# Opening each PSUM bank once, and adding the norm's transposes onto a shift that ACT writes

## The chip, the cores and the metric

The kernel runs on one core of a Trainium2 chip. The time is the device time of that core in microseconds (us); the median of several runs is given. The core's engines are PE (TensorE, matrix products and transposes), DVE (VectorE), ACT (ScalarE), POOL (GpSimd) and SP (SyncE, which issues the DMAs here). Each runs its own queue in order and waits for the others through semaphores. PE writes its results to PSUM, which has eight banks; POOL does not touch PSUM.

## The reference

The input `x` is 128 x 32 x 256 (batch, time, features), the condition 128 x 256. Two layers follow each other. All that the change touches is in the first, and in the norm at the head of the second:

```
# layer 0: a recurrence over the 32 time steps (RK4, state q and p of 128 x 256, q0 = p0 = cond)
dq = q - q**3/3 - p + x[:, t] + tanh(q) @ coupling.T + bias      # four times a step
dp = 0.08 * (q + 0.7 - 0.8 * p)
q, p = clip(q + DT/6*(dq1 + 2*dq2 + 2*dq3 + dq4)), clip(...)
# its FFN on every step's q: block-quantized, 256 -> 1024 -> 256
x1 = x + mx_linear(silu(mx_linear(q, w_gate)) * mx_linear(q, w_up), w_down)

# layer 1: norm with scale and shift from the condition, then attention and a ternary FFN
scale, shift = split(cond @ W_emb + b_emb, 2)                    # 128 x 256 each: per batch row
xn = x1 * rsqrt(mean(x1*x1) + 1e-6) * g_norm * (1 + scale) + shift
out = x1 + ffn1(attention(xn @ W_qkv))
```

The batch has 128 rows, so a time step's state fills the 128 partitions once.

## The kernel before, in words

**Phases.** Phase one goes over the 32 time steps: `step(t)` (line 604) is the recurrence, `ffn0(t)` (line 915) the first FFN and the norm of that step. Phase two goes over 32 groups of 128 tokens (`tokens(g)`, line 1134) and starts with products of `xnT`, the transposed norm that phase one leaves behind.

**Order of the work.** Nothing is issued where it is written. Each function calls `work.add(engine, cost, fn, reads, writes, ...)`; the class `Work` (lines 100 to 341) then plans all queues with these costs (list scheduling, run to and fro for up to 40 rounds, phase one first and then phase two from the engine times that phase one ends with), and `emit` (line 1366) issues the items in that order. Buffers (`Buf`) are given slots of a pool by the planner as they come free. `keep_warm` (line 321) looks for planned gaps of PE over 0.45 us and puts products of zeros (line 1375) into them, into a buffer whose first writer is a later item of PE.

**The recurrence in a step.** Four stages, each with an accumulator `ps[i]` in PSUM: `ps[0]` and `ps[2]` are the same slot, `ps[1]` and `ps[3]` the other; each slot has a bank of its own (line 413). A stage's accumulator is first opened by `opened` (line 519), a PE product of zeros with the start flag and no stop flag, 128 x 256 in bf16. Then DVE (`nest`, line 577) or, for the fourth, ACT (line 661) writes start values over it, and PE adds onto them: `plus` (line 612) adds a scaled buffer through a scaled identity, and `slope` has ACT compute tanh and square (lines 619, 620), PE the product with the coupling (line 626) and POOL the cube (line 633). DVE then reads the sum (`nest`, `add_sat`, line 672).

**The FFN and the norm of a step.** The state is transposed into `ps_turn` (line 551), quantized (lines 708, 929, 909 on DVE, 935 on POOL), turned by DMA (line 457), multiplied with gate and up (line 950), combined (958, 962), quantized again (708, 977, 909, 985), and turned by DMA. The down product goes into `po`, in a bank of its own: `opened(po)`, ACT writes the residual `x` (line 993), and eight products add onto it (line 997). ACT copies it out as `x1` (line 1003) and sums its squares (line 1009), POOL takes the power (line 1015). For the first 27 steps ACT then scales (line 1020), POOL multiplies with the gain (line 1024) and adds the shift (line 1028); for the last five (`LATE`) DVE does both (lines 1033, 1035). PE transposes the result into `px`, one of two slots in the bank `ps_turn` (line 1036), and ACT copies it into `xnT` (line 1038). The other users of `ps_turn` in each step are the state's transpose `pt` (line 920) and the transpose `pd` of the next `x` (line 591), which ACT reads (line 597).

**Gain and shift** are made once in `modulation` (line 823): PE multiplies the transposed condition with both halves of `W_emb` (line 831), and DVE adds the bias to each half (lines 837, 839).

Of the kernel before, what the change touches and what calls it, by code (L numbers as in the profile page):

```python
# [14 lines left out]
AF = mybir.ActivationFunctionType  # L15
# [5 lines left out]
P = 128  # L21
# [18 lines left out]
PE, DVE, ACT, POOL, SP = "PE", "DVE", "ACT", "POOL", "SP"  # L40
# [305 lines left out]
def kernel(  # L346
# [22 lines left out]
    nc = tc.nc  # L369
    B, T, N = x.shape  # L370
    FF = w0_gate.shape[0]
    NC = N // P
    FC = FF // P
# [22 lines left out]
    mid = slots("mid", HALF, 10)  # L396
    slim = slots("slim", N, 18)
# [8 lines left out]
    def banks(name, n, count):  # L406

        tiles = [ps_1.tile([P, HALF], F32, name=f"{name}{i}") for i in range(-(-count * n // HALF))]
        return [
            Slot(t[:, k : k + n], f"{name}{i}") for i, t in enumerate(tiles) for k in range(0, HALF, n)  # L410
        ][:count]

    ps_stage = [banks(f"ps_stage{i}", N, 1) for i in range(2)] * 2
    ps_po = banks("ps_po", N, 1)
    ps_sum = banks("ps_sum", N, 4)
    shared = ps_sum.pop()
    n_tiny = FF // BLOCK
# [7 lines left out]
    def fixed(name, shape, dtype=F32):  # L425

        b = Buf(())
        t = tile_of(name, shape, dtype)
        b.slots, b.slot = [Slot(t)], 0
        return b, t  # L430
# [30 lines left out]
    def two(ap):  # L461
        return ap.rearrange("p (c k) -> p c k", c=NC)

    def load(slots_, src, rank, as_=None, after=()):
        b = Buf(slots_)
        add(
            SP, 0.45, lambda: nc.sync.dma_start(as_(b.ap) if as_ else b.ap, src),
            fills=[b], rank=rank, tail=4.0 if slots_ is raws else 1.8, after=after,
        )
        return b  # L470
# [17 lines left out]
    b_oh, w_oh = fixed("w_oh", [P, NC, N])  # L488
    b_gp, g_prod = fixed("g_prod", [P, D_HEAD])
    b_gain, gain = fixed("gain", [P, N])  # L490
    b_shift, shift = fixed("shift", [P, N])
    b_xnT, xnT = fixed("xnT", [P, NC, B, T])
    xnT_flat = xnT.rearrange("p c b t -> p c (b t)")
    x1_dram = dram.tile([B, T, N], F32, name="x1_dram")
# [21 lines left out]
    zeros = tile_of("zeros", [P, N], BF16)  # L516
    nc.gpsimd.memset(zeros, 0.0)

    def opened(dst, rank, after=()):
        add(  # L520
            PE, 0.11,
            lambda: nc.tensor.matmul(dst.ap, lhsT=zeros[:, :P], rhs=zeros, start=True, stop=False),
            [], [dst], rank=rank, after=after,
        )


# [21 lines left out]
    def turn(dst, src, n=NC):  # L548
        for c in range(n):
            sl = slice(c * P, (c + 1) * P)  # L550
            nc.tensor.transpose(dst[:, sl], src[:, sl], ident)  # L551
# [52 lines left out]
    def step(t, q, p, d):  # L604
        rank = t - 500.0
        ps = [Buf(slots_) for slots_ in ps_stage]
        x, w, z = Buf(ps_sum), Buf(ps_sum), p
        q2, q3, m4, w2, qn = Buf(slim), Buf(slim), Buf(slim), Buf(slim), Buf(states)

        def plus(i, eye, src, cost=0.43):  # L610
            return add(
                PE, cost, lambda: nc.tensor.matmul(ps[i].ap, lhsT=eyes[eye], rhs=src.ap, start=False, stop=False),  # L612
                [src], [ps[i]], rank=rank,
            )

        def slope(i, qi):

            th, sq = Buf(slim), Buf(slim)
            add(ACT, 0.32, lambda: nc.scalar.activation(th.ap, qi.ap, AF.Tanh, scale=1.0 / S3 if i == 2 else 1.0), [qi], [th], rank=rank, table="silu")  # L619
            add(ACT, 0.31, lambda: nc.scalar.activation(sq.ap, qi.ap, AF.Square, scale=CUBES[i]), [qi], [sq], rank=rank)  # L620

            def mm():
                for c in range(NC):
                    for m in range(NC):
                        sl = slice(m * P, (m + 1) * P)
                        nc.tensor.matmul(  # L626
                            ps[i].ap[:, sl], lhsT=coup[i][:, c, sl], rhs=two(th.ap)[:, c, :],
                            start=False, stop=(c == NC - 1 and m == NC - 1),
                        )

            add(PE, 0.9, mm, [th, b_coup[i]], [ps[i]], rank=rank)
            add(
                POOL, 0.685, lambda: nc.gpsimd.tensor_tensor(sq.ap, sq.ap, qi.ap, MULT),  # L633
                [qi], [sq], rank=rank, port=True,
            )
            return sq

        for i in range(2):
            opened(ps[i], rank)
            nest(ps[i], p, -h / 2 * (1.0, P2[0])[i] * S / K[i], q, rank)  # L640
            if not i:
                started.append(work.items[-1])
            plus(i, i, d)
        nest(x, p, -h * P3[0] * S / K[2], q, rank)
        cube = slope(0, q)
        nest(w, p, LAST[0] * S / LAST[1], q, rank)
        nest(z, p, END[0] * S / END[1], q, rank)
        nest(q2, ps[0], K[0], cube, rank, SUB)
        plus(1, 1, q2)
        cube = slope(1, q2)  # L650
        opened(ps[2], rank)
        nest(ps[2], q2, -h * P3[2] / K[2], x, rank)
        plus(2, 2, d)
        nest(w, d, h / 6 / LAST[1], w, rank)
        nest(w2, w, LAST[1] / LAST[2], q2, rank)
        nest(z, z, END[1] / END[2], q2, rank)
        nest(q3, ps[1], K[1] * S3, cube, rank)
        plus(2, 6, q3)
        cube = slope(2, q3)
        opened(ps[3], rank)  # L660
        add(ACT, 0.27, lambda: nc.scalar.mul(ps[3].ap, w2.ap, LAST[2]), [w2], [ps[3]], rank=rank)
        plus(3, 4, q3)
        nest(z, z, END[2] / S, q3, rank)
        nest(m4, ps[2], -K[2], cube, rank, SUB)
        plus(3, 5, m4)
        cube = slope(3, m4)
        edge = ALPHA / BETA

        def add_sat(dst, in0, in1, low, high):
            add(  # L670
                DVE, 0.335,
                lambda: nc.vector._custom_dve(TENSOR_ADD_SAT, out=dst.ap, in0=in0.ap, in1=in1.ap, s0=high, s1=low),
                [b for b in (in0, in1) if b is not dst], [dst], rank=rank,
            )

        add_sat(z, z, m4, (CLAMP - edge) / S, (-CLAMP - edge) / S)
        add_sat(qn, ps[3], cube, -CLAMP, CLAMP)
        return qn, z
# [143 lines left out]

    def modulation(rank):
        emb = [load(mid, w_emb[c * P : (c + 1) * P, :], rank) for c in range(NC)]
        b_e = load(mid, b_emb.partition_broadcast(P), rank)
        g_n = load(slim, g_norm.partition_broadcast(P), rank)
        pe = Buf(ps_gu)

        def mm():
            for c in range(NC):  # L830
                nc.tensor.matmul(
                    pe.ap, lhsT=two(condT)[:, c, :], rhs=emb[c].ap, start=(c == 0), stop=(c == NC - 1)
                )

        add(PE, 1.72, mm, [b_condT, *emb], [pe], rank=rank)
        tt = nc.vector.tensor_tensor
        add(DVE, 0.335, lambda: tt(gain, pe.ap[:, :N], b_e.ap[:, :N], ADD), [pe, b_e], [b_gain], rank=rank)
        add(DVE, 0.335, lambda: stt(gain, gain, 1.0, g_n.ap, ADD, MULT), [g_n], [b_gain], rank=rank, port=True)
        add(DVE, 0.335, lambda: tt(shift, pe.ap[:, N:], b_e.ap[:, N:], ADD), [pe, b_e], [b_shift], rank=rank)

    def constants_of_phase_two(rank):

# [72 lines left out]
    def ffn0(t, q):  # L915
# [72 lines left out]
                [b8, bscl], fills=[bq], rank=rank, port=True,  # L988
            )
        turned(bT, bq, FF, rank)  # L990
        po, x1, ms, xn, px = Buf(ps_po), Buf(slim), Buf(tiny), Buf(slim), Buf(ps_turn)
        opened(po, rank)
        add(ACT, 0.31, lambda: nc.scalar.copy(po.ap, xt.ap), [xt], [po], rank=rank)

        def down():
            for c in range(FC):
                nc.tensor.matmul(
                    po.ap, lhsT=bT.ap[:, c * P : (c + 1) * P], rhs=w0dT[:, c, :],
                    start=False, stop=(c == FC - 1),
                )  # L1000

        add(PE, 0.88, down, [bT, b_w0d], [po], rank=rank)
# [15 lines left out]
        if t < T - LATE:  # L1018
            add(
                ACT, 0.42, lambda: nc.scalar.activation(xn.ap, po.ap, AF.Copy, scale=m1()),  # L1020
                [po, ms], [xn], rank=rank,
            )
            add(
                POOL, 0.685, lambda: nc.gpsimd.tensor_tensor(xn.ap, xn.ap, gain, MULT),
                [b_gain], [xn], rank=rank, port=True,
            )
            add(
                POOL, 0.685, lambda: nc.gpsimd.tensor_tensor(xn.ap, xn.ap, shift, ADD),
                [b_shift], [xn], rank=rank, port=True,
            )  # L1030
        else:
            add(
                DVE, 0.335, lambda: stt(xn.ap, po.ap, m1(), gain, MULT, MULT), [po, ms, b_gain], [xn], rank=rank
            )
            add(DVE, 0.335, lambda: tt(xn.ap, xn.ap, shift, ADD), [b_shift], [xn], rank=rank, port=True)
        add(PE, 0.22, lambda: turn(px.ap, xn.ap), [xn], [px], rank=rank)
        xnT_done.append(
            add(ACT, 0.4, lambda: nc.scalar.copy(xnT[:, :, :, t], two(px.ap)), [px], fills=[b_xnT], rank=rank)
        )
# [398 lines left out]
```

## Time and profile before

| | |
|---|---|
| Three runs | 836.7, 838.51, 838.08 us; median 838.08 |
| The profiled execution | span 839.5 us from the first to the last instruction; its time outside the span is not given |
| Phase one, to the last copy into `xnT` | 418.5 us |
| Phase two | 421.0 us |
| Busy over the span | PE 93%, DVE 86%, POOL 73%, ACT 60% |
| Products of zeros by `opened` | 160 (128 into the stages, 32 into `po`) |
| Products of zeros by `keep_warm` | 219 |

How to read it: a line such as `L1028 POOL TENSOR_TENSOR slim<-slim,shift` names the line of the kernel, the engine, the operation, and out<-in by buffer names without their numbers. `L577` is the helper `nest`, `L551` the helper `turn` and `L522` the products of `opened`. A matmul of fp32 operands is two records; a transpose is one. Matmuls overlap in time, so that a busy PE is not a PE at its limit. A wait line says which engine and line stood for which other.

### The profile page before, as it was taken

The numbers are of one execution on the slowest core, as the hardware profiler recorded it, in microseconds if no ns is written. First come the engines' busy times: TensorE is split into PE (matmuls) and PEld (weight loads), VectorE is DVE, ScalarE is ACT, GpSimd is POOL, SyncE is SP. The second block draws the span as 40 slices with busy tenths as digits, with TensorE's granted clock in tenths as the row PEclk, the third lists the DMA queues.
The fourth block names the chain that finished last, engine by engine and source line by source line (L and its number), as shares of the span: only waits on it lengthen the run. The fifth ranks groups of instructions, "written<-read, shape, count | busy, mean of one in ns | idle before, by whom it ended". The sixth has DMA issues, their size and how long they took to land.

```text
span 839.5 us, 26212 instructions
## 1 busy us (share of the span) xinstructions
PE 783.7 (93%) x10455; PEld 583.7 (70%) x10455; DVE 721.1 (86%) x1848; ACT 507.3 (60%) x1021; POOL 610.0 (73%) x956
## 2 busy tenths in 40 slices
PE   7889999999999999998688999999999999999996
PEld 4666677777777877775455576777767676778675
DVE  4998999999999999999368698979898889888794
ACT  3225456655656665696533676767668576765864
POOL 5787998988798988889555677785773877867320
PEclk9999999999999999999799999999999999999999
DMA  7312232323132343255300021133223122231333
GB/s 229 107 39 48 59 77 61 83 60 70 51 71 70 70 139 65 57 130 127 78 2 7 16 44 50 40 71 65 57 37 57 40 49 53 37 62 34 75 83 76
DMA packets 128891, 55.53 MB, mean 66 GB/s; under 512 B 102144, under 2 KB 127616, under 8 KB 128768
## 3 DMA queue, kind: packets, MB, share of 16 engines
q1 hardware_dynamic: 128768, 53.85, 28.0%
q8 instruction: 82, 1.34, 0.7%
q14 instruction: 41, 0.34, 0.1%
HBM read 21.32 MB, written 8.39 MB: 35 GB/s over the span
## 4 chain that ended last, share of the span: by engine, by line
PE 29%; DVE 17%; POOL 6%; ACT 5%; DMA 4%; issue 4%; ACTq 0%; SPq 0%; DVEq 0%; POOLq 0%
PE ps_two L1284 4%; PE ps_one L1146 4%; PE ps_two L1326 3%; DVE wide L1315 3%; DVE tiny L1092 2%; DMA wide_bf<-wide_bf 2%; PE ps_one L1228 2%; POOL wide L1315 2%; PE ps_one L1198 2%; PE ps_stage L626 2%; PE ps_one L1349 2%; PE ps_stage L612 2%; PE ps_two L551 2%; PE ps_one L1153 2%; DVE wide L1299 1%
## 5 line engine op out<-in xcount | busy, mean ns | idle before, releaser
L1315 POOL TENSOR_TENSOR wide<-wide 128x512 f32<-128x512 f32 x116 | 148.2, 1298 | 62.9 <-DVE wide L1315 24.8
L626 PEld LDWEIGHTS ps_stage<-slim,coup 128*128 128x128 f32 x1024 | 128.7, 192 | 19.0 <-ACT slim L619 11.2
L626 PE MATMUL ps_stage<-slim,coup 128*128 128x128 f32 x1024 | 139.2, 279 | 0.3
L633 POOL TENSOR_TENSOR slim<-slim,slim 128x256 f32<-128x256 f32 x96 | 72.6, 756 | 23.0 <-ACT slim L620 16.5
L612 PE MATMUL ps_stage<-slim,eye 128*128 128x256 f32 x256 | 80.0, 396 | 4.8 <-DVE slim L577 3.7
L619 ACT ACTIVATE slim<-slim 128x256 f32<-128x256 f32 x96 | 39.4, 410 | 51.7 <-DVE slim L577 51.7
L977 POOL TENSOR_TENSOR mid<-mid,tiny 128x512 f32<-128x512 f32 x64 | 66.6, 1050 | 4.8 <-DVE tiny L698 4.7
L985 POOL TENSOR_TENSOR wide_bf<-mid,tiny 128x512 bf16<-128x512 fp8e4 x64 | 66.9, 1051 | 4.1 <-DVE mid L909 3.9
L1326 PE MATMUL ps_two<-had_ffn,wide 128*128 128x128 f32 x512 | 63.7, 278 | 2.0 <-ACT wide L1321 1.1
L620 ACT ACTIVATE slim<-slim 128x256 f32<-128x256 f32 x96 | 39.1, 407 | 42.9 <-DVE slim L577 40.8
L1326 PEld LDWEIGHTS ps_two<-had_ffn,wide 128*128 128x128 f32 x512 | 60.3, 192 | 6.0 <-ACT wide L1321 2.6
L612 PE MATMUL ps_stage<-drives,eye 128*128 128x256 f32 x192 | 60.5, 398 | 2.8 <-DVE ps_stage L577 2.1
L1146 PE MATMUL ps_one<-w_qkv_sb,xnT 128*128 128x512 f32 x128 | 61.4, 603 | 0.4 <-ACT v_pad L1162 0.2
L1315 DVE TENSOR_TENSOR wide<-wide 128x512 f32<-128x512 f32 x76 | 57.4, 778 | 1.3 <-POOL wide L1315 1.3
L1292 ACT ACTIVATE mid<-ps_two,tiny 128x512 f32<-128x512 f32 x64 | 43.4, 687 | 23.7 <-PE ps_two L1284 23.3
L612 PEld LDWEIGHTS ps_stage<-slim,eye 128*128 128x128 f32 x256 | 39.5, 189 | 25.5 <-DVE slim L577 19.5
L1228 PEld LDWEIGHTS ps_one<-v_pad,mid 32*32 32x32 f32 x4096 | 40.8, 105 | 22.3 <-issue 17.4
L1299 DVE SCALAR_TENSOR_TENSOR wide<-ps_two,tiny,mid 128x512 f32<-128x512 f32 x64 | 46.9, 741 | 9.2 <-ACT mid L1292 8.5
L1334 ACT ACTIVATE wide<-ps_two,magic,tiny 128x1024 f32<-128x1024 f32 x32 | 38.6, 1205 | 26.0 <-DVE tiny L1100 21.8
L1228 PE MATMUL ps_one<-v_pad,mid 32*32 32x17 f32 x4096 | 46.7, 181 | 3.2 <-DVE mid L1221 1.8
L1092 DVE TENSOR_REDUCE tiny<-ps_two 128x1 f32<-128x1024 f32 x32 | 38.6, 1206 | 8.9 <-PE ps_two L1326 8.8
L962 DVE TENSOR_TENSOR mid<-ps_gu,mid 128x512 f32<-128x512 f32 x64 | 43.6, 682 | 2.3 <-PE ps_gu L950 1.7
(169 smaller groups left out, 2151.1 us busy)
## 6 DMA issues: line engine op xcount, KB each, us to landing
x_step<-in_x_dram SPq DMA_DIRECT2D x32, 128.0 KB, 2.1
x_add<-in_x_dram SPq DMA_DIRECT2D x32, 128.0 KB, 2.1
x_dram<-slim SPq DMA_DIRECT2D x32, 128.0 KB, 1.7
slim<-x_dram SPq DMA_DIRECT2D x32, 128.0 KB, 2.4
out_dram<-slim SPq DMA_DIRECT2D x32, 128.0 KB, 1.9
raws<-in_L_ffn_w_gate_dram SPq DMA_DIRECT2D x4, 512.0 KB, 4.8
raws<-in_L_ffn_w_up_dram SPq DMA_DIRECT2D x4, 512.0 KB, 6.1
raws<-in_L_ffn_w_down_dram SPq DMA_DIRECT2D x4, 512.0 KB, 5.0
```

The source lines that it names most:

```text
L612: PE, cost, lambda: nc.tensor.matmul(ps[i].ap, lhsT=eyes[eye], rhs=src.ap, start=False, stop=False),
L626: nc.tensor.matmul(ps[i].ap[:, sl], lhsT=coup[i][:, c, sl], rhs=two(th.ap)[:, c, :], start=False, stop=(c == NC - 1 and m == NC - 1),)
L633: POOL, 0.685, lambda: nc.gpsimd.tensor_tensor(sq.ap, sq.ap, qi.ap, MULT),
L962: DVE, 0.6, lambda act=act, it=it, pu=pgu[1]: tt(it.ap, pu.ap, act.ap, MULT),
L977: lambda it=it, ks=ks: nc.gpsimd.tensor_tensor(blocks(it.ap), blocks(it.ap), spread(binv.ap[:, ks], BLOCK), MULT),
L985: lambda b8=b8, ks=ks, sl=sl: nc.gpsimd.tensor_tensor(blocks(bq.ap[:, sl]), blocks(b8.ap), spread(bscl.ap[:, ks], BLOCK), MULT),
L1092: lambda: nc.vector.tensor_reduce(am.ap[:, 0:1], src.ap[:, :n], AX.X, ALU.max, apply_absolute_value=True),
L1146: nc.tensor.matmul(pqk.ap, lhsT=xnT_flat[:, c, tok], rhs=w_qkv_sb[:, c, : 2 * N], start=(c == 0), stop=(c == NC - 1),)
L1228: nc.tensor.matmul(by_v(po.ap)[row, hd, :], lhsT=by_head(exT.ap)[row, hd, :], rhs=v_pad.ap[row, hd, :], start=True, stop=True,)
L1299: lambda pgu=pgu, act=act, sl=sl: stt(it.ap[:, sl], pgu.ap[:, HALF:], sgu.ap[:, 1:2], act.ap, MULT, MULT),
L1315: eng.tensor_tensor(dv[:, :, e, :], sv[:, :, 0, :], sv[:, :, 1, :], op)
L1326: nc.tensor.matmul(pfh.ap[:, sl], lhsT=iT.ap[:, sl], rhs=had_ffn, start=True, stop=True)
```

## The change

1. `opened` goes, with its 160 planned products. Four products of zeros are issued ahead of all planned work instead: one for each of the two stage banks and one for each half of the `po` bank. The first three have the start flag; the fourth, in the same bank as the third, has not. The products that add onto these banks keep `start=False` and now have the stop flag.
2. `px` moves from a slot of `ps_turn` to the second half of the bank of `po`, where it has one slot of its own.
3. The shift is kept transposed (`[P, NC, B]`). In `modulation` PE makes it transposed with four products, ACT adds the bias (loaded one value to a partition by a small DMA), and the DVE addition goes; the bias that is broadcast to all partitions is only the gain's half.
4. In `ffn0` the addition of the shift on POOL or DVE goes. ACT copies the transposed shift into `px`, and the two transposes of the norm, with `start=False`, add onto it. The copy into `xnT` is as before.

```diff
-    ps_po = banks("ps_po", N, 1)
+    ps_po, ps_px = ([slot] for slot in banks("ps_po", N, 2))
...
-    b_shift, shift = fixed("shift", [P, N])
+    b_shift, shift = fixed("shift", [P, NC, B])
+    b_be, shift_bias = fixed("shift_bias", [P, NC])
...
-    def opened(dst, rank, after=()):
-        add(
-            PE, 0.11,
-            lambda: nc.tensor.matmul(dst.ap, lhsT=zeros[:, :P], rhs=zeros, start=True, stop=False),
-            [], [dst], rank=rank, after=after,
+    for slot in (ps_stage[0][0], ps_stage[1][0], ps_po[0], ps_px[0]):
+        nc.tensor.matmul(
+            slot.ap, lhsT=zeros[:, :P], rhs=zeros, start=slot is not ps_px[0], stop=True, skip_group_check=True
         )
...
-                PE, cost, lambda: nc.tensor.matmul(ps[i].ap, lhsT=eyes[eye], rhs=src.ap, start=False, stop=False),
+                PE, cost, lambda: nc.tensor.matmul(ps[i].ap, lhsT=eyes[eye], rhs=src.ap, start=False, stop=True, skip_group_check=True),
...
-                            start=False, stop=(c == NC - 1 and m == NC - 1),
+                            start=False, stop=True, skip_group_check=True,
...
         for i in range(2):
-            opened(ps[i], rank)
             nest(ps[i], p, -h / 2 * (1.0, P2[0])[i] * S / K[i], q, rank)
...
-        opened(ps[2], rank)
         nest(ps[2], q2, -h * P3[2] / K[2], x, rank)
...
-        opened(ps[3], rank)
         add(ACT, 0.27, lambda: nc.scalar.mul(ps[3].ap, w2.ap, LAST[2]), [w2], [ps[3]], rank=rank)
...
     def modulation(rank):
         emb = [load(mid, w_emb[c * P : (c + 1) * P, :], rank) for c in range(NC)]
-        b_e = load(mid, b_emb.partition_broadcast(P), rank)
+        b_e = load(slim, b_emb[:N].partition_broadcast(P), rank)
+
+        def load_shift_bias():
+            with nc.allow_non_contiguous_dma(reason="256 elements, one per partition and chunk"):
+                nc.sync.dma_start(shift_bias, b_emb[N:].rearrange("(c p) -> p c", p=P))
+
+        add(SP, 0.45, load_shift_bias, fills=[b_be], rank=rank, tail=1.8)
...
-                    pe.ap, lhsT=two(condT)[:, c, :], rhs=emb[c].ap, start=(c == 0), stop=(c == NC - 1)
+                    pe.ap[:, :N], lhsT=two(condT)[:, c, :], rhs=emb[c].ap[:, :N], start=(c == 0), stop=(c == NC - 1)
...
-        add(PE, 1.72, mm, [b_condT, *emb], [pe], rank=rank)
+        add(PE, 0.86, mm, [b_condT, *emb], [pe], rank=rank)
+        for m in range(NC):
+            pm = Buf(ps_gu)
+
+            def mm_shift(pm=pm, m=m):
+                for c in range(NC):
+                    nc.tensor.matmul(
+                        pm.ap[:, :P], lhsT=emb[c].ap[:, N + m * P : N + (m + 1) * P], rhs=two(condT)[:, c, :],
+                        start=(c == 0), stop=(c == NC - 1),
+                    )
+
+            add(PE, 0.45, mm_shift, [b_condT, *emb], [pm], rank=rank)
+            add(
+                ACT, 0.27,
+                lambda pm=pm, m=m: nc.scalar.activation(
+                    shift[:, m, :], pm.ap[:, :P], AF.Identity, bias=shift_bias[:, m : m + 1]
+                ),
+                [pm, b_be], fills=[b_shift], rank=rank,
+            )
...
-        add(DVE, 0.335, lambda: tt(shift, pe.ap[:, N:], b_e.ap[:, N:], ADD), [pe, b_e], [b_shift], rank=rank)
...
-        po, x1, ms, xn, px = Buf(ps_po), Buf(slim), Buf(tiny), Buf(slim), Buf(ps_turn)
-        opened(po, rank)
+        po, x1, ms, xn, px = Buf(ps_po), Buf(slim), Buf(tiny), Buf(slim), Buf(ps_px)
...
-                    start=False, stop=(c == FC - 1),
+                    start=False, stop=True, skip_group_check=True,
...
-            add(
-                POOL, 0.685, lambda: nc.gpsimd.tensor_tensor(xn.ap, xn.ap, shift, ADD),
-                [b_shift], [xn], rank=rank, port=True,
-            )
...
-            add(DVE, 0.335, lambda: tt(xn.ap, xn.ap, shift, ADD), [b_shift], [xn], rank=rank, port=True)
-        add(PE, 0.22, lambda: turn(px.ap, xn.ap), [xn], [px], rank=rank)
+        add(ACT, 0.27, lambda: nc.scalar.copy(two(px.ap), shift), [b_shift], [px], rank=rank)
+
+        def onto_shift():
+            for c in range(NC):
+                sl = slice(c * P, (c + 1) * P)
+                nc.tensor.matmul(
+                    px.ap[:, sl], lhsT=xn.ap[:, sl], rhs=ident, is_transpose=True,
+                    start=False, stop=True, skip_group_check=True,
+                )
+
+        add(PE, 0.22, onto_shift, [xn], [px], rank=rank)
```

More of the change, by code (lines that the diff above doesn't have):

```diff
@@ L831, in mm @@
                 nc.tensor.matmul(
-                    pe.ap, lhsT=two(condT)[:, c, :], rhs=emb[c].ap, start=(c == 0), stop=(c == NC - 1)
+                    pe.ap[:, :N], lhsT=two(condT)[:, c, :], rhs=emb[c].ap[:, :N], start=(c == 0), stop=(c == NC - 1)
                 )
-        add(PE, 1.72, mm, [b_condT, *emb], [pe], rank=rank)
+        add(PE, 0.86, mm, [b_condT, *emb], [pe], rank=rank)
[15 more added lines that the diff above has]
+            )
         tt = nc.vector.tensor_tensor
-        add(DVE, 0.335, lambda: tt(gain, pe.ap[:, :N], b_e.ap[:, :N], ADD), [pe, b_e], [b_gain], rank=rank)
+        add(DVE, 0.335, lambda: tt(gain, pe.ap[:, :N], b_e.ap, ADD), [pe, b_e], [b_gain], rank=rank)
         add(DVE, 0.335, lambda: stt(gain, gain, 1.0, g_n.ap, ADD, MULT), [g_n], [b_gain], rank=rank, port=True)
-        add(DVE, 0.335, lambda: tt(shift, pe.ap[:, N:], b_e.ap[:, N:], ADD), [pe, b_e], [b_shift], rank=rank)
     def constants_of_phase_two(rank):
```

## The prediction, made before the changed kernel ran

> **What bounds the kernel now.** I read the windows first, cut at the kernel's own events: the 7th and the 28th write of `states` (107.3 and 341.2 us in the timeline), the 32nd (387.3), and the last `xnT` copy (418.5), where phase one ends.
>
> ```profile
> core 0: us, PE busy (x) PEld busy (x) DVE busy (x) ACT busy (x) POOL busy (x), PEclk, DMA share, GB/s
> 107.30:341.20 233.90, 230.66 (x1536) 180.69 (x1534) 224.42 (x641) 140.71 (x401) 205.41 (x279) 1.00 0.32 72
> 387.30:418.50 31.20, 20.68 (x109) 12.35 (x109) 17.62 (x48) 21.46 (x43) 21.70 (x31) 0.78 0.52 115
> 418.50:839.50 421.00, 393.54 (x7993) 289.83 (x7992) 343.86 (x812) 271.27 (x382) 257.82 (x500) 1.00 0.23 48
> ```
>
> To be seen: in the middle, 21 steps take 233.9 us, 11.14 us each, and PE (99%), DVE (96%) and POOL (88%) are all nearly full; ACT is 60% busy. The change touches phase one alone; phase two, 421 us, keeps its instructions.
>
> Busy time overstates PE, because matmuls overlap. So next I took start-to-start times from runs of like instructions, in the chain of work that ended last:
>
> ```profile
> 299.34 0.89 PE ps_stage L626 x8
> 324.97 0.88 PE ps_gu L950 x4
> 356.33 0.87 PE ps_po L997 x8
> ```
>
> That is 0.111, 0.22 and 0.109 us a record. L612 comes to 0.215 (two last 0.60 in the timeline, one 0.39). By the counts of the groups over 32 steps, PE needs 32 x 0.111 + 14 x 0.215 (L612) + 8 x 0.22 + 8 x 0.109 + 6 x 0.11 (transposes) + 5 x 0.11 (the products of zeros, L522) = **10.4 us a step**. On DVE, neighbours overlap by 0.085 us (two L577 last 0.75, one 0.42): 18 operations of 256 columns at 0.336, 6.15 of 512 at 0.594 and 6.1 small ones at 0.086 make **10.2 us**. POOL is busy 9.8 us a step. The step is thus 1.071 times the fullest engine, which is PE, with DVE close behind.
>
> Then the waits, DVE's alone, in the same stretch, whole lines (us in total, times, longest):
>
> ```profile
> DVE states L672 <- POOL slim L633: 1.0, 2, 0.7
> DVE ps_stage L577 <- PE ps_stage L522: 1.0, 1, 1.0
> DVE states L672 <- PE ps_stage L522: 0.6, 2, 0.3
> DVE tiny L708 <- ACT drives L597: 0.3, 1, 0.3
> DVE slim L929 <- ACT drives L597: 0.2, 1, 0.2
> ```
>
> DVE is idle only 9.5 us in 233.9, and the zeros end 1.6 us of that by name. No single wait is there to be removed; what can be had is slack. The last two lines matter for a rival: L708 and L929 read the transposed state, L597 the transposed drive, in another slot of the same bank, and yet they wait for each other. A bank, not a slot, is handed from engine to engine.
>
> **What the skill says.** (1) "PSUM — Partial Sum Buffer", The four PSUM rules: a matmul with the start flag clears the has-written bits of its whole bank, later matmuls add where the bit is set, and ACT and DVE writes leave the bits alone. So one product per bank can serve all steps, as long as nothing later starts a group there. No row of this trace shows the bits. (2) The same page, PSUM bank collisions: two engines must not be in one bank at once, so a kernel has to guard by bank; the two waits just shown agree. (3) "TensorE: Matmul & The Clock Gate", Wait — 56ns, not 53.3ns?: a warm matmul costs N/2.4 GHz plus 2.5 ns, 0.109 us for 256 columns; the trace agrees (0.87 us for eight). (4) The same page, What's actually happening: after an idle window of about 3.4 us the array's clock is halved; the granted clock of 0.78 from 387.3 to 418.5 us agrees in kind.
>
> **The change, part by part.** The rows it rests on, from the groups (busy us, mean ns, then idle before):
>
> ```profile
> L522 PE MATMUL ps_stage<-zeros 128*128 128x256 bf16 x128 | 34.9, 274 | 4.7 <-DVE states L672 2.3 <-POOL zeros L517 1.8 <-DVE slim L577 0.2
> L522 PE MATMUL ps_po<-zeros 128*128 128x256 bf16 x32 | 9.1, 285 | 0.1
> L1028 POOL TENSOR_TENSOR slim<-slim,shift 128x256 f32<-128x256 f32 x27 | 19.7, 729 | 0.6
> L1035 DVE TENSOR_TENSOR slim<-slim,shift 128x256 f32<-128x256 f32 x5 | 2.4, 473 | 0.1
> L993 ACT COPY ps_po<-x_add 128x256 f32<-128x256 f32 x32 | 12.1, 380 | 9.4 <-PE ps_po L522 9.4
> ```
>
> *Zeros.* 160 products become 4, once, at the start. PE's need falls by 5 x 0.11 = 0.55 to 9.85 us a step. A hop DVE to PE to DVE also goes where a stage's bank is reused (1.6 us of DVE waits). ACT's 9.4 us before L993 go too, but ACT has room: worth nothing.
>
> *Shift.* 27 POOL additions of 0.729 us leave POOL: 9.8 to 9.1 us a step. Five DVE additions of 0.473 us leave the last five tokens. 32 ACT copies into PSUM come in, at L993's 0.38 us. What hides them is ACT's idle time, 93 us of the 234; without that cover they cost about 0.29 us (a copy less its overlap) x 27 = 8 us. I take 0: ACT's long waits are for DVE before tanh and square (33.4 us at L619 in the stretch), and the shift copy needs nothing but its own earlier `xnT` copy. Queued behind it on ACT are tanh and square, and PE's L626 waits for those.
>
> *Transposes that add.* No row shows a transpose onto seeded data. Lower bound: today's record of 0.109 us (a gain is excluded, the same columns pass); upper bound: that it runs like the fp32 product L626, two records of 0.111 us for 128 columns, +0.23 us of PE a step. I take 0; even at +0.23 PE stays under DVE.
>
> *Moved bank.* `px` leaves the bank of the state's and drive's transposes and enters that of `po`. This relieves DVE's readers of `ps_turn`, and adds handovers between ACT and PE in `po`'s bank. I take 0 net; the bad end is the rival below.
>
> *Stop flags.* They add no instruction: 0.
>
> *Modulation, once.* PE's four records of 1.057 us (L831) have half the columns for the gain; two pairs for the shift are added, two ACT activations (0.36 us, as L597) take the place of one DVE addition (0.415 us), and SP issues one more small load (0.43 us for the alike `bias_sb`) ahead of `g_norm`'s. DVE stood 5.2 us for L831's first reader, so this may give up to 2 us or, if the loads line up worse, cost 1.5. I take 0.
>
> *The order.* The planner lays all queues anew. Phase two starts from other engine times, so even its order may differ; I allow 3 us either way and take 0.
>
> **Sum.** After the change DVE is the fullest engine. If the queues stay as well packed, a step takes 10.2 x 1.071 = 10.93 us instead of 11.14: 0.21 us less, in the 25 steps from 107.3 to 387.3 us: -5.3 us. Before 107.3 the weights' quantization fills DVE and nothing is gained. In the tail the chain reads:
>
> ```profile
> 409.79 3.23 DMA wide_bf<-wide_bf
> 413.07 1.89 PE ps_po L997 x8
> 414.95 2.52 PE ps_turn L1375 x12
> 417.47 0.40 PE ps_turn L551 x2
> 417.89 0.60 ACT xnT L1038
> ```
>
> Between the down product and the last transpose stand accumulation, power, L1033 and L1035 (the products of zeros of L1375 only fill). L1035 goes from that end: 0.5 us; another at 403.63 us stood ahead of the scales: some 0.2 more. What is late next there is L1033, which waits for POOL's power. Together -5.3 - 0.7 = **-6.0 us**. The profiled execution's span is 839.5 us, 1.4 over the runs' median; its time outside the span is not shown. The same difference from 838.08 gives **832 us**.
>
> **Rivals.** *Nothing paid in the steps* (0.15): DVE keeps its pace, since only 1.6 us of its waits name the zeros; the tail's 0.7 us and the noise of a new order remain: 837, from 835 to 840. For it speaks that DVE is 96% busy; against it, that a fixed order on three full engines loses time to each of them.
> *The bank blocks PE* (0.18): slower. Place: PE's queue at the new transposes and at the next token's down product. PE must not enter `po`'s bank while ACT copies the shift in (0.38 us) or `xnT` out (0.61 us), and the planner knows slots, not this handover. It decides from the 0.55 us a step that the zeros give back. If both copies stop PE, it needs 9.85 + 0.99 = 10.84, times 1.071 = 11.61: +0.47 x 25 - 0.7 = +11 us, 849; with the `xnT` copy alone 10.46, 11.20, +1 us. I put it at 845. Against it: `po`'s bank has eleven us a step for about four us of tenants, and the same handovers leave `ps_turn`.
> *A deeper gain* (0.10): less on PE and POOL also frees DVE's order, and half of the 0.94 us between step and DVE's need goes: 0.47 x 25 + 0.7 = 12.5 us, 825.6.
> *A colder tail* (inside the ranges): the filling products can only go into a buffer that PE opens; `px`, `po` and the stages are now opened by DVE or ACT, so the twelve at 414.95 have no place. Phase two then starts colder: 0 to 1.7 us, half of the first eight L1146 records' 3.44.
>
> **The numbers.** Forecast -3 to -9 us, 829 to 835, chance 0.57. The range 824 to 841 leaves out most of the blocking case and the end of the deep one. A measurement of this kernel tells about 0.2%, 1.7 us, from no change. Forecast and deep gain are faster (0.67), and a little of the second case; its middle and the edge of the blocking case are the same: faster 0.69, same 0.13, slower 0.18.
>
> **What would show it.** L522's rows gone but for four products; 21 middle steps in about 229.5 us with DVE near 97% and PE's count 105 lower; POOL's L1028 gone; `xnT`'s last copy near 412. Wrong if that stretch keeps its length, if PE waits for `xnT` or shift copies by more than 0.5 us a step, or if the difference sits in phase two.

## The result, and the profile after

The changed kernel takes 840.27 us (median of 20 runs, 836.5 to 844.22), beside 838.97 us for the kernel before on the same chip (20 runs). The ratio is 1.0011, 95% interval 0.9993 to 1.0029: no difference that the runs can tell, where 832 us was forecast. A second set gave 839.93 us and 1.0001 [0.9982, 1.0019]. Every ratio below is to the kernel before as it ran beside the kernel in question; the times themselves come from several sets, in which the median of before lay between 838.22 and 840.85 us.

The kernel did not stand still; two stages moved against each other. Here are the windows of the profile after, cut at the same events as before (7th and 28th write of `states`, the 32nd, the last `xnT` copy). The columns are as before: busy us and instruction counts of PE, PEld, DVE, ACT, POOL, then PE's granted clock, DMA share and GB/s.

```profile
105.50:336.70 231.20, 226.33 (x1454) 172.84 (x1452) 224.12 (x653) 151.78 (x437) 194.35 (x265) 1.00 0.33 76
380.80:417.80 37.00, 19.05 (x112) 12.38 (x110) 17.53 (x46) 26.12 (x52) 23.24 (x33) 0.76 0.62 120
417.80:842.10 424.30, 397.84 (x7993) 291.47 (x7992) 344.09 (x812) 270.91 (x383) 257.90 (x500) 0.99 0.23 47
```

The first line is the good news: 21 steps in 231.2 us instead of 233.9, DVE 97% busy. The second is the bad news: the tail, from the last state to the last `xnT` copy, has grown from 31.2 to 37.0 us, though PE is busy in it for less time and the clock is much the same. All stages, in us, each from one profiled execution:

| | to the 7th state | 7th to 28th | 28th to 32nd | tail | phase two | span |
|---|---|---|---|---|---|---|
| before | 107.3 | 233.9 | 46.1 | 31.2 | 421.0 | 839.5 |
| after | 105.5 | 231.2 | 44.1 | 37.0 | 424.3 | 842.1 |
| after, second set | 105.6 | 231.5 | 43.9 | 37.1 | 421.0 | 839.1 |

The 32nd state comes 6.5 us earlier; the last `xnT` copy only 0.7 us earlier. The tail gives back 5.8 us. The 3.3 us of phase two in the first row of after belong to that one execution, the longest of its set: the second has 421.0, as before.

The rows of the new operations, in the groups of after (busy us, mean ns, then the idle time ahead of them and what ended it):

```profile
L1042 POOL TENSOR_TENSOR slim<-slim,gain 128x256 f32<-128x256 f32 x27 | 19.6, 727 | 0.2 <-ACT slim L1038 0.2
L1054 PE MATMUL ps_po<-ident,slim 128*128 128x128 f32 x64 | 13.7, 298 | 6.9 <-ACT ps_po L1011 4.2 <-DVE slim L1047 2.5 <-ACT slim L1021 0.2
L1049 ACT COPY ps_po<-shift 128x256 f32<-128x256 f32 x32 | 12.1, 378 | 2.8 <-PE ps_po L1015 2.0
L521 PE MATMUL ps_stage<-zeros 128*128 128x256 bf16 x2 | 0.6, 421 | 0.0
```

In these rows L1042 is the multiplication with the gain, L1049 the shift copy, L1054 the transposes that add onto it, L1011 the copy of the residual `xt` into `po`, L1015 the down product, L1027 the sum of squares and L1061 the copy into `xnT`. Of POOL's two passes over the norm only the gain is left. A transpose that adds onto the shift is one record, as a plain one is. The shift copy takes ACT 0.378 us, and the products of zeros are down to four (two here, two into `ps_po`). New is what ends the transposes' idle time: ACT's L1011, the copy of `xt` into `po`. That is another token's tenant of the same bank. The waits within the tail of after (total us, times, longest):

```profile
PE ps_po L1015 <- ACT ps_po L1049: 5.2, 2, 3.1
PE ps_po L1054 <- ACT ps_po L1011: 4.2, 2, 3.0
ACT slim L1027 <- PE ps_po L1054: 2.5, 2, 1.4
PE ps_po L1015 <- ACT xnT L1061: 0.7, 1, 0.7
```

None of these four is a need of the data. The down product (L1015) has no use for a shift copy, nor the transposes (L1054) for `xt`, nor the square (L1027) for another token's transposes. That they stand for each other fits that both slots lie in one bank; run 6 tests it. In the tail of before, PE's transposes and down products waited for ACT too, but 5.5 us instead of the 10.1 of the three PE lines here:

```profile
PE ps_turn L551 <- ACT xnT L1038: 4.7, 4, 2.3
PE ps_po L997 <- ACT ps_po L993: 0.8, 1, 0.8
```

The chain of work that ended last shows the same, in order of time (start, us, what); here is its part ahead of the last token's down product:

```profile
409.07 0.94 ACT wide_bf L813
410.01 0.28 ACT ps_po L1049
410.32 0.39 ACT ps_po L1011
...
410.75 0.70 PE ps_po L1054 x2
411.52 0.60 ACT xnT L1061
...
412.16 1.88 PE ps_po L1015 x8
```

The last down product, eight records at 412.16, comes behind an ACT copy of a shift, an ACT copy of `xt`, another token's transposes and that token's `xnT` copy, each in the one bank. Its data did not hold it: the first of its weights, a part of the transposed hidden, was loaded at 411.02 us, 1.1 us before the product began. In the tail of before, quoted in the prediction, the product started when its transposed hidden had landed. The 1.88 us of after's product also show the halved clock (the third number from the end of each line):

```profile
400.00:405.00 5.00, 2.21 (x10) 1.55 (x10) 0.99 (x2) 3.82 (x8) 1.89 (x4) 0.53 0.09 28
405.00:410.00 5.00, 2.29 (x10) 1.43 (x9) 0.48 (x1) 3.61 (x8) 2.55 (x5) 0.50 0.55 107
410.00:417.80 7.80, 3.24 (x12) 1.83 (x13) 0.48 (x1) 2.94 (x9) 0.75 (x2) 0.50 0.27 67
```

PE is less than half busy by these windows, and nothing fills its gaps. In before, filling products go into `ps_turn` until 417.1 us; in after, the last one ahead of the tail's end stands at 395.6, since no buffer of the norm is opened by PE any more.

### The profile page after: what moved, and what is told of

Its sections match the earlier page's. It is cut to its first block, busy times and chain, and to the rows that moved or that the text cites. A ratio compares the mean times of both kernels' runs of the same rounds, so it can differ in the third digit from the quotient of the medians.

```text
span 842.1 us, 25876 instructions
## 1 busy us (share of the span) xinstructions
PE 773.1 (92%) x10306; PEld 573.1 (68%) x10306; DVE 714.5 (85%) x1842; ACT 517.2 (61%) x1055; POOL 589.8 (70%) x929
## 4 chain that ended last, share of the span: by engine, by line
PE 47%; DVE 26%; ACT 9%; POOL 7%; issue 6%; DMA 5%; ACTq 0%; SPq 0%; DVEq 0%; POOLq 0%
PE ps_stage L625 8%; PE ps_stage L611 7%; PE ps_one L1169 5%; PE ps_two L1307 4%; PE ps_gu L969 3%; PE ps_two L1349 3%; DVE tiny L1115 3%; DVE wide L1338 3%; PE ps_po L1015 3%; DVE slim L576 2%; PE ps_one L1221 2%; DVE ps_sum L576 2%; PE ps_one L1251 2%; DMA wide_bf<-wide_bf 2%; PE ps_one L1176 2%
## 5 line engine op out<-in xcount | busy, mean ns | idle before, releaser
L625 PEld LDWEIGHTS ps_stage<-slim,coup 128*128 128x128 f32 x1024 | 131.0, 194 | 18.6 <-ACT slim L618 12.0
L611 PE MATMUL ps_stage<-slim,eye 128*128 128x256 f32 x256 | 82.0, 402 | 8.3 <-DVE slim L576 7.8
L618 ACT ACTIVATE slim<-slim 128x256 f32<-128x256 f32 x96 | 39.3, 410 | 43.9 <-DVE slim L576 43.7
L611 PE MATMUL ps_stage<-drives,eye 128*128 128x256 f32 x192 | 62.7, 410 | 2.5 <-DVE ps_stage L576 1.6
L1169 PE MATMUL ps_one<-w_qkv_sb,xnT 128*128 128x512 f32 x128 | 64.1, 626 | 0.4 <-ACT v_pad L1185 0.2
L1315 ACT ACTIVATE mid<-ps_two,tiny 128x512 f32<-128x512 f32 x64 | 43.5, 688 | 23.9 <-PE ps_two L1307 23.6
L611 PEld LDWEIGHTS ps_stage<-slim,eye 128*128 128x128 f32 x256 | 38.9, 189 | 28.0 <-DVE slim L576 26.5
```

Of the source, the lines that this page charges most:

```text
L625: nc.tensor.matmul(ps[i].ap[:, sl], lhsT=coup[i][:, c, sl], rhs=two(th.ap)[:, c, :], start=False, stop=True, skip_group_check=True,)
L1169: nc.tensor.matmul(pqk.ap, lhsT=xnT_flat[:, c, tok], rhs=w_qkv_sb[:, c, : 2 * N], start=(c == 0), stop=(c == NC - 1),)
```

## The experiments

**The theory** after this profile: the zeros pay what was forecast, and the shift's place takes it back in the tail, through the bank that `px` now shares with `po`, and through PE's clock. **Rivals**: the planner's new order happens to be better in the middle and worse at the end; or the shift half costs in every step. In all kernels below the lines move by a few.

**1 and 2. Each half alone.** *zeros_only* is the kernel before, with `px` and POOL's or DVE's addition of the shift as they were, and

```
-    def opened(dst, rank, after=()): ... start=True, stop=False
+    for slot in (ps_stage[0][0], ps_stage[1][0], ps_po[0]):
+        nc.tensor.matmul(slot.ap, lhsT=zeros[:, :P], rhs=zeros, start=True, stop=True, ...)
```

> The first half of the change alone: the 160 opening products become one per bank; the shift is added as before and the transposed norm stays in ps_turn. Bank theory (the tail lost its gain because the norm's transposes share po's bank): the steps gain as in the changed kernel and the tail keeps its 31 us, so phase one ends near 414 and the time is about 834 us. Fixed-tail rival (weights' work and DMAs of the tail end when they end): the last state comes earlier, but phase one still ends near 417 to 418, time about 838.

Measured: 835.69 us, ratio 0.9943 [0.9921, 0.9966]. *shift_only* is the changed kernel with the products of zeros planned again for the stages and for `po` (for `po` without the start flag, as `px` may be live in the bank).

> The second half alone: seeded shift and px in po's bank, with the opening products still planned (those of po without the start flag, so that they only add zeros). Bank theory: the tail from the last state to the last xnT copy is about 36 us instead of 31, with PE and ACT waiting for each other across po and px, and the time is 840 to 844 us. Fixed-tail rival: phase one ends near 418, time about 839.

Measured: 865.09 us, ratio 1.0298 [1.024, 1.0355]; middle 240.3 us, tail 45.4, far above both expectations. So the zeros alone gain and the shift alone loses. Yet neither is clean: both orders are laid anew, and the gain of zeros_only doesn't sit in the middle steps (236.4 us, longer than before's), but at the start (104.1 us to the 7th state instead of 107.3), in the last four steps (44.2 instead of 46.1) and in the tail (27.8 instead of 31.2).

**3. The zeros in the order of before.** In *zeros_same_order* the planner still plans the opening products, but PE doesn't issue them:

```
-            lambda: nc.tensor.matmul(dst.ap, lhsT=zeros[:, :P], rhs=zeros, start=True, stop=False),
+            lambda: None,
```

> The kernel before with its own order of every queue, in which the 160 opening products are planned but not issued (one product per bank at the start). Slack theory of the prediction: PE is 93% occupied, so 0.55 us less a step shortens the 21 middle steps from 233.9 us to about 229, and the time falls by 4 to 6 us to 833 to 835. Replanning rival: with the order kept, the products were covered, the middle stretch stays within 1 us of 233.9 and the time within 2 us of the kernel before; what zeros_only won came from another order.

Measured: 836.84 us, ratio 0.9934 [0.9905, 0.9963], which is -5.5 us of 838 (the medians of that set, 840.85 and 836.84, give -4.0). In the windows the middle has 231.0 us, 2.9 less than before, though not the 229 expected; the tail has 29.0:

```profile
106.30:337.30 231.00, 226.58 (x1429) 170.53 (x1430) 223.83 (x640) 138.22 (x400) 204.67 (x279) 1.00 0.31 73
```

The order is that of before, so this is the worth of PE's slack and not of a new order. Set beside after (231.2 us, POOL busy 194.35 us instead of 204.67), it suggests that the shift half does little in the steps, either through the 10 us that POOL is relieved of or through the bank. It doesn't show it, because after has an order of its own.

**4 and 5. What does a new order alone do?** *replan_a* and *replan_b* are the kernel before with the planner told 0.10 or 0.13 us for an opening product in place of 0.11. Every queue is laid anew; the instructions stay, apart from fillers.

> The kernel before, same instructions, but the planner is told 0.10 us instead of 0.11 for an opening product, so that it lays other queues. Replanning rival: the time differs from the kernel before by 3 us or more either way, and the stages (start, middle, tail) differ by as much as those of the changed kernel did. Slack theory: within 2 us.

> The same with 0.13 us. Replanning rival: again another order, and 3 us or more from the kernel before or from replan_a. Slack theory: within 2 us of both.

Measured: 845.2 us, 1.0064 [1.0032, 1.0097], and 841.38 us, 1.0004 [0.9983, 1.0025]. A new order alone moved the time by up to 0.6%, 5 us: as much as the whole effect in question, so that only runs in one and the same order can be laid side by side in single microseconds.

**6. The bank, in the order of after.** *late_place* keeps every queue of after and moves `px` of the last seven tokens to the free half of the second stage's bank, which is idle at that time:

```
+        px_ap = lambda: px_late.ap if t >= T - 7 else px.ap
-        add(ACT, 0.27, lambda: nc.scalar.copy(two(px.ap), shift), [b_shift], [px], rank=rank)
+        add(ACT, 0.27, lambda: nc.scalar.copy(two(px_ap()), shift), [b_shift], [px], rank=rank)
```

(the transposes and the `xnT` copy likewise).

> The changed kernel with the same order of every queue; only px of the last seven tokens lies elsewhere in PSUM, in the free half of a stage's bank, which is idle by then. Bank theory: the waits of L1054-like transposes for the residual copy and of the down products for shift and xnT copies (17 us by name in the tail) go, the tail falls from 36 to about 31 us, and the time is about 835 us. Fixed-tail rival: no change against the changed kernel, 840 us.

Measured: 837.28 us, ratio 0.9976 [0.9957, 0.9994], which is 3.0 us under the median of after; middle 230.9, tail 32.3 instead of 37.0. Its chain of work shows what stands before the last down product now:

```profile
401.40 0.39 ACT ps_po L1018
401.79 0.30 ACT ps_stage L1056
402.08 0.60 ACT wide_bf L819
402.68 3.59 DMA wide_bf<-wide_bf
406.27 0.05 issue
406.32 1.90 PE ps_po L1022 x8
```

L1018, L1056 and L1022 are after's L1011, L1049 and L1015. The product starts when its data has landed, and waits for no copy: 27.0 us after the 32nd state (379.3) instead of 31.4 in after. So the shared bank is shown as a cause of the long tail. In the run time the intervals of late_place and after just touch. The gain is smaller than expected (the tail was to fall to 31 us, the time to 835), for two reasons that the trace gives. PE's waits for ACT don't vanish; in place of the 10.1 us in after it now waits 6.7 us for copies that it needs, those of the residual and of the shift for the same token:

```profile
PE ps_po L1022 <- ACT ps_po L1018: 3.6, 2, 2.6
PE ps_stage L1061 <- ACT ps_stage L1056: 3.1, 2, 2.5
```

And the tail's granted clock has risen as well, from 0.76 to 0.82, so the 4.7 us are not the waits alone.

**7. The clock, in the order of after.** *warm_tail* lets the planner's `keep_warm` put its zeros into the first stage's buffer in the tail's gaps as well, 36 more products, with `px` where the change put it:

```
+            if not item.warm and item.rank < self.SECOND and prev.start > self.free_from.end:
+                item.warm = (self.spare, int(0.5 * gap / 0.11))
```

> The changed kernel with the same order, and 36 more filling products of zeros in PE's gaps after the last state, into the first stage's bank. Cold-PE theory: the granted clock stays whole through tail and start of phase two; the down products in the tail last 1.0 instead of 1.9 us, phase two loses its 3 us, and the time is about 836 us. Bank theory: the tail falls by about 1 us only, time 838 to 840.

Measured: 837.86 us, ratio 1.0001 [0.998, 1.0022]; tail 34.7. In its chain two of the three last down products run at the full clock, for 1.03 and 1.05 us instead of 1.86 and 1.88:

```profile
403.66 1.03 PE ps_po L1017 x8
...
409.07 1.05 PE ps_po L1017 x8
```

The stage is 2.3 us shorter, at a granted clock of 0.95. In the whole time that can't be told from after; neither expectation was met in full, as the time is not shown to fall and the tail falls by more than 1 us.

**8 and 9. Both repairs together**, in two sets. *place_warm* and *place_warm_again* are one kernel, 6 and 7 in one.

> The changed kernel in the same order with both repairs: px of the last seven tokens in a stage's bank, and the filling products in the tail. If bank and cold PE are separate causes, their gains add: 3.0 us (late_place) and about 2.4 us (warm_tail) under the changed kernel's 840.3, so about 835 us, the tail near 30 us. If they are one and the same (PE cold because it waits for the bank), about 837.

> Both repairs together once more, in more rounds. If they pay for the two costs found in the tail: 833 to 836, ratio to the kernel before 0.990 to 0.995, tail near 31.5 us. If the earlier 834.8 was chance: 837 to 840, ratio above 0.997.

Measured: 834.75 us, 0.9909 [0.9879, 0.9939], and 833.73 us, 0.9911 [0.9884, 0.9938]. It beats before and after alike, by 7.5 us of 838 for before. The tail, 37.0 us in after:

```profile
379.60:411.00 31.40, 21.00 (x148) 14.65 (x147) 17.53 (x47) 25.40 (x52) 23.34 (x33) 0.95 0.73 141
```

In the tail the two gains overlap: 4.7 us by the move, 2.3 by the warming, but 5.6 by both (5.5 in place_warm) and not 7.0. At one and the same clock, 0.95, the move alone takes the tail from 34.7 us (warm_tail) to 31.4 or 31.5. So 3.2 to 3.3 us are the bank's with the clock held; with the move made, warming is worth 0.8 to 0.9 us. In the run time the move is clear of the noise here: 1.0001 [0.998, 1.0022] without it (warm_tail), 0.9911 [0.9884, 0.9938] with it.

**10. After once more**, beside 9 and 11.

> The changed kernel once more, beside the next two. Both theories: within 0.3% of the kernel before (838 to 842). If its profiled execution falls on a shorter one, the stretch from the 32nd state to the last xnT copy should still be near 37 us (36 to 38), since the waits inside the bank of po are of the order; if that stretch comes out near 32, the tail of the first profile was an accident of one execution and the bank theory loses its main number.

Measured: 839.93 us, tail 37.1. The long tail is no accident of one execution.

**11. The same move for the slow half.** *shift_place* is shift_only with the edit of late_place.

> The shift alone with its opening products (the slow one, 865), with px of the last seven tokens in the free half of the second stage's bank, in the same order. If the handover in the bank of po is what makes its tail 45.4 us long, the tail falls to about 33 us and the time by about 12 us to 853; if the length lies in the new order alone, tail and time stay within 3 us of 45 and 865. The middle stretch (240 us) should stay in both cases, as nothing in it moves.

Measured: 860.47 us, 1.0224 [1.0181, 1.0267]; tail 41.0 instead of 45.4, middle 240.4 as before the move. Neither expectation was met. The move accounts for 4.4 us of that tail (its granted clock rises from 0.73 to 0.80), about as much as in after, and not for the 12 expected. The greater part of the 26 us that shift_only loses lies elsewhere: 6.4 us in the middle stretch and some 10 in a tail with ten tokens left. It isn't settled here whether its own order or the new products of zeros in `po`'s bank, which wait for ACT in turn, are the cause. In shift_only's tail these products wait 6.4 us for ACT by name, in its middle 0.5 us, so these waits don't account for the longer middle. shift_only is therefore no measure of the shift half.

**12 to 14. Is the long tail the draw of one order?** The changed kernel, with the planner told another cost for the shift copy:

```
-        add(ACT, 0.27, lambda: nc.scalar.copy(two(px.ap), shift), [b_shift], [px], rank=rank)
+        add(ACT, 0.25, ...)   # replan_after_a;  0.30: replan_after_b;  0.38: replan_after_c
```

> The changed kernel with its instructions unchanged, except that the planner is told 0.25 us for the shift copy in place of 0.27, so that all queues are laid anew. If the long tail belongs to px in the bank of po, the tail is again long (over 34 us) and the time 835 to 845; if the tail of 37 us was the draw of one order, the tail falls to 28 to 33 us (as the orders of the kernel before gave: 31.2, 32.5, 30.9, 29.0, 27.8) and the time follows the middle stretch alone.

> The same with 0.30 us for the shift copy. Bank theory: tail over 34 us. Rival, the draw of one order: tail 28 to 33 us. The middle stretch should fall between 229 and 239 us either way, the spread that new orders of the kernel before showed.

> The same with 0.38 us for the shift copy, which is what the copy takes in the profile. Bank theory: tail over 34 us. Rival, the draw of one order: tail 28 to 33 us.

Measured: 848.71 us (1.0127 [1.0079, 1.0175]), 852.86 us (1.0174 [1.0133, 1.0214]) and 840.68 us (1.0022 [1.0003, 1.0041]). By where `px` lives, the orders that were laid (shift_only apart, whose tail of 45.4 us holds opening products too), with PE's granted clock in the tail and the tokens whose norm is still to be written out after the 32nd state:

| `px` in | kernel | middle, us | tail, us | clock in it | tokens in it |
|---|---|---|---|---|---|
| `ps_turn` | before | 233.9 | 31.2 | 0.78 | 10 |
| `ps_turn` | zeros_only | 236.4 | 27.8 | 0.94 | 7 |
| `ps_turn` | replan_a | 238.8 | 32.5 | 0.84 | 11 |
| `ps_turn` | replan_b | 234.6 | 30.9 | 0.89 | 9 |
| `po`'s bank | after | 231.2 | 37.0 | 0.76 | 8 |
| `po`'s bank | replan_after_a | 233.0 | 38.9 | 0.71 | 7 |
| `po`'s bank | replan_after_b | 233.5 | 43.9 | 0.72 | 8 |
| `po`'s bank | replan_after_c | 232.6 | 35.2 | 0.71 | 7 |

The tails don't overlap: 27.8 to 32.5 us in the one bank (mean 30.6), 35.2 to 43.9 in the other (mean 38.8), with seven or eight tokens left against seven to eleven. So the long tail comes with the change and not with a draw. Which part of the change it is, the table doesn't tell: the clock separates the two groups as well, 0.78 to 0.94 in the one and 0.71 to 0.76 in the other, and with `px` out of `ps_turn` the filling products lose their place at the norm's transposes. Runs 6 to 9 tell it, in one order. The waits in the longest of these tails carry the same names as in after:

```profile
PE ps_po L1054 <- ACT ps_po L1011: 4.6, 2, 2.4
PE ps_po L1015 <- ACT ps_po L1049: 3.6, 2, 2.8
```

The bank theory had also expected 835 to 845 us for replan_after_a, which took 848.71. Of the four orders of the changed kernel, the one that it came with and replan_after_c are the best; the other two are slower than before beyond doubt. The four lie 12.6 us apart, though their tails differ by only 8.7. So "no change" holds for the order that the change came with, one of the two best of four, and not for the change under any order.

## Why the prediction was wrong

**The zeros' slack: right in the whole, two thirds of the size in a step.** Forecast were -5.3 us from the 7th to the 32nd state. After has 280.0 to 275.3, -4.7; zeros_same_order 280.0 to 276.3, -3.7, and another 2.2 in the tail, which was not forecast. The price "0.21 us a step" measured 0.13 (11.01 us in after, 11.00 in zeros_same_order, against 11.14). In the run time the zeros give -0.66% [-0.95, -0.37], 5.5 us, nearly all of the 6.0 forecast. The kernel rests on what the Trainium skill says ("PSUM — Partial Sum Buffer", The four PSUM rules), that the bits stay set until the next product with the start flag in that bank. No row of a trace shows the bits; the traces show that the four products at the start (L521) are the only ones left for all 32 steps.

**The failed step: "I take 0 net" for the moved bank.** In the steps nothing speaks against it: PE's waits for `xnT` copies in `po`'s bank are 0.5 us over the whole middle of after, not the 0.5 us a step of the blocking rival. The tail was not priced at all. There seven or eight tokens' norms are bunched, so that token t's shift copy, transposes and `xnT` copy interleave with the next token's `xt` copy and down product, and each handover puts a chain of ACT copies before a PE product that has its data. "Eleven us a step for about four us of tenants" is an average over the steps and says nothing of it. In the order of after the handover is worth 4.7 us of the tail, 3.2 to 3.3 of it with the clock held, and 2 to 3 us of the time (late_place, 0.9976, beside after's 1.0011 and 1.0001).

**"A colder tail", mis-sized.** It was seen that the twelve filling products would have no place, but the loss was looked for at the start of phase two, as 0 to 1.7 us. It falls inside the tail, where warming gives 2.3 us back with `px` in `po`'s bank, and 0.8 to 0.9 us with `px` moved. This is what the halved clock costs after, not what the change added: the tail of before is at half clock for 13.6 us as well (stretches of 3.4 and 10.2), that of after for 17.5 (part of one of 20.5 that reaches into phase two). The part that is the change's own was not measured; as before's tail was cold too, it should be less than these 2.3 us.

**"Tail -0.7" failed.** L1035 did go from that end, but instead of L1033's power the bank came in as what is late next: +5.8 us. -4.7 in the steps, -1.8 before them (not forecast, within what a new order moves), +5.8 in the tail: -0.7 at the end of phase one.

**The rival on the slower side** had the mechanism and the two instructions right, PE's queue at the new transposes and at the next down product, and the place wrong: it charged every step, where only the tail pays. With hindsight, a rival priced at the tail alone, with the 5.8 us that the profile shows against the zeros' -5.5, would have given "no change".

**Taken at nothing:** for the transposes onto seeded data rightly so, as their record shows. For POOL's relief and the shift copies on ACT (12.1 us) no mark is seen on the middle, 231.2 us beside 231.0 without them, in another order. In the tail the shift copies do count: they stand in the chain, in late_place too (0.30 us at 401.79). **"The order: 3 us either way"** was too small: replan_a moved the kernel before by 5 us, and the four orders of the changed kernel lie 12.6 us apart. With this spread, that the changed kernel came out level with before, and not slower, is in part luck.

**What stays open.** Both repairs together bring the kernel to 0.991, within the -3 to -9 us that were forecast, so repairs made in the tail alone recover what the forecast missed, though warming also mends some cold that before had. But warming on top of the move gained more in the run time (0.9909 and 0.9911 against 0.9976) than the 0.8 to 0.9 us by which it shortens that tail; the rest isn't located. So the shares of bank and clock are known in the tail, not in the whole. Why replan_after_a and replan_after_b are slower than after by more than their tails isn't explained. The loss of shift_only is not explained. That place_warm beats the zeros alone isn't shown either: 0.9911 [0.9884, 0.9938] and 0.9934 [0.9905, 0.9963] overlap, so the shift half, even repaired, has no proven worth.

## What to carry over

When a buffer moves to another PSUM bank, look for its new neighbours in the stage where the work bunches, at the end or the start of a pipeline, and not at the mean load of the bank. The planner here knows slots but not this handover, and put tenants side by side there. Where an operation changes which engine opens a buffer, ask what else used that opening, here the products that keep PE's clock up. And where queues are laid by a planner, measure a change in the old order too, or over several orders: a new order alone moved the kernel before by 0.6%, and four orders of the changed kernel lie 1.6% apart.

## What the runs showed of the hardware

- An fp32 transpose that adds onto 128x256 values that ACT had copied into PSUM costs PE what a plain one costs: one record, 273 ns median in both kernels (L1054 in after, L551 into `ps_turn` in before).
- The half-clock stretches of PE, apart from those that the end of a trace cuts off, come in multiples of one length: 3.4, 6.8, 10.2, 13.7, 17.1, 20.5, 23.9 and 27.3 us in the traces of this study. The Trainium skill ("TensorE: Matmul & The Clock Gate", What's actually happening) gives a window of about 3.4 us; the traces agree with its length.
- 36 products of zeros in the tail's gaps raised its granted clock from 0.76 to 0.95 and shortened eight records of a down product there from 1.86 to 1.03 us.
- Two slots of one bank, with tenants of two tokens that ACT fills, PE adds to and ACT reads, cost 3.2 to 3.3 us of a tail of 34.7 us at the same granted clock (warm_tail beside place_warm and place_warm_again).
